# Three moves in the recurrent stage of a two-layer graph kernel

## Chip, cores and metric

One core of a Trainium2 chip runs the whole program. The metric is the device time in microseconds of one execution; the profile shows one such execution, engine by engine. The engines are TensorE (PE in the profile; its weight loads PEld), VectorE (DVE), ScalarE (ACT), GpSimd (POOL) and SyncE (SP), which here only issues DMAs.

## The reference

16 graphs of 1024 nodes, 128 features and a dense 1024 x 1024 adjacency matrix. A layer norm with a ReLU goes ahead of each of two networks, and each result is added to its input. The first network, in which the change lies, is a gated recurrent one of four layers:

```python
for i in range(L):                                   # L = 4
    hw = jnp.einsum('bnc,cd->bnd', h, weight[i])
    m = jnp.einsum('bjn,bjd->bnd', adj, hw)
    h = _gru_cell(m, h, w_ih[i], w_hh[i], b_ih[i], b_hh[i])

# _gru_cell, with gx = m @ w_ih.T + b_ih and gh = h @ w_hh.T + b_hh, each split in three
r = jax.nn.sigmoid(xr + hr)
z = jax.nn.sigmoid(xz + hz)
n = jnp.tanh(xn + r * hn)
return (1.0 - z) * n + z * h
```

The second network has four layers of adjacency times features times weights, a ReLU and a batch norm over all graphs.

## The kernel before

The first network takes about 1170 us of the span, the second the rest. In the first, two streams, `sa` with the even graphs and `sb` with the odd ones, are worked alternately. `half_step(one, two)` (L1035) does two things on TensorE: the gates of stream `two` for its layer (`gate_step(0)` and `gate_step(1)`, a half of 512 nodes each), and then the aggregation over the adjacency matrix of stream `one` (`agg_step(0)` and `agg_step(1)`). `one.i` and `two.i` are the layers at which the streams stand. Both streams need eight half steps for a pair of graphs; seven times a new pair is taken.

The aggregation (L525) multiplies exact adjacency rows with features split in two: a high part, rounded to the matmul's type, and a low part, the remainder. For each block of 128 nodes the two high matmuls come first and the two low ones next, so both parts of a half are wanted at the start. From layer 1 on the features are the state h, which must first be turned by 128 x 128. This is done without TensorE: VectorE turns 32 x 32 blocks (`half_away`, L711, tile `t_h`), SP writes the half to DRAM (`exchange_out`, L591, `cross_h`) and reads it back in four DMAs in the other order of blocks (`exchange_in`, L598, `n_h`), ScalarE makes the high part (`split_back`, L905, `ghw`), VectorE the low part (L906).

In the gates, ScalarE makes r (L984), VectorE two steps of the candidate (L985, L986), ScalarE its tanh (L990) and z (L991), and VectorE three steps of the new h (L995 or L997, L998, L999). z needs the last of the six matmuls of a half. `m` is the aggregation's result, copied by ScalarE (L944).

After its fourth layer a stream takes its next graph (`finish`, L1004). Then the new features `y` and the last state h both go through the same exchange: they are written away at once, and read back in the half step after, `ins` (the new features) at its start, `outs` (the last h, eight DMAs `h<-cross_out`) after the first half of the gates. The last h read back is summed with x under a mask at L732 for the second network's layer norm; the sums, the normed blocks (`y_mid`) and the blocks of the coming graph (`y_in`, `next_blocks`, L818, eight ScalarE instructions from L674) run as work for the gap between the two halves of an aggregation ("gap" in the agenda, `at` and `due`).

The order on TensorE, GpSimd and SP is that of the program text. On ScalarE and VectorE a scheduler puts the instructions in order when the program is built, with durations of its own; `behind(x)` tells it to put what is in its scope behind x, and is an order in the queue, not a wait. `split_back` puts the high part behind the z of the first half, and nothing puts it ahead of or behind the z of the second.

GpSimd rounds adjacency rows (`row`) and casts them to 16 bits (L609, `half`); SP turns these by DMA transposes (L610, `adjT<-half`), and two `half` buffers make the next cast wait for a transpose.

Of the kernel before, what the change touches and what calls it, by code (L numbers as in the profile page):

```python
# [8 lines left out]
F32 = mybir.dt.float32  # L9
# [4 lines left out]
AF = mybir.ActivationFunctionType  # L14
ALU = mybir.AluOpType
AX = mybir.AxisListType
P = 128
# [324 lines left out]
def exact_path(  # L342
# [21 lines left out]
    nc = tc.nc  # L364
    B, N, C = x.shape
    L = g_weight.shape[0]
    NB = N // P
    NH = N // HALF
    BH = HALF // P
# [164 lines left out]
    with ExitStack() as st:  # L534
# [137 lines left out]
        def norm_blocks(xt, y, nt, ks):  # L672
            for k in ks:
                nc.scalar.activation(  # L674
                    y[:, k * P : (k + 1) * P], xt[:, k, :], AF.Relu, bias=nt[3][:, k, :], scale=nt[2][:, k, :]
                )
# [84 lines left out]
        def behind(*inss):  # L761

            es = ExitStack()
            for ins in () if written[0] else inss:
                es.enter_context(tc.issue_after(ins.ins))
            return es

        class Stream:
# [46 lines left out]
            def next_factors(self):  # L815
                norm_factors(self.next_norm)

            def next_blocks(self):  # L818
                self.next_y = work.tile([P, N], F32, tag=f"y{self.tag}", name=f"y_in{self.b + 2}", bufs=1)
                norm_blocks(self.next_x, self.next_y, self.next_norm, range(NB))  # L820

            def plan(self, n, tail=None):

                if tail:
                    b, xt, hT, parts = tail
                    end = {}

                    def sums():
                        end["norm"] = tail_sums(b, xt, hT, parts)

                    def blocks():
                        end["y"] = y_mid(b)
                        norm_blocks(xt, end["y"], end["norm"], range(NB))

                    at(n + 2, "gap", sums)
                    at(n + 3, "mid", lambda: store_xmid(b, xt))
                    at(n + 3, "gap", lambda: norm_factors(end["norm"]))
                    at(n + 4, "gap", blocks)
                    at(n + 5, "mid", lambda: store_ymid(b, end["y"]))
                if self.b + 2 < B:  # L840
                    at(n + 5, "mid", self.next_load)
                    at(n + 5, "gap", self.next_sums)
                    at(n + 6, "gap", self.next_factors)
                    at(n + 7, "gap", self.next_blocks)

            def fetch(self):
# [105 lines left out]
                hin = self.hT[:, :HALF]  # L952
                nc.tensor.matmul(self.opened[2], w_hhT[:, 0, 2 * C : 3 * C], hin, start=True, stop=True)

            def gate_step(self, hf, between=None, after=()):
                i, nm = self.i, f"{self.b}_{self.i}_{hf}"
                if hf == 0 and not self.opened:
                    self.new = work.tile([P, N], F32, tag="h", name=f"h{nm}", bufs=7)
                cols = slice(hf * HALF, (hf + 1) * HALF)
                hin, m = self.hT[:, cols], self.m[hf]  # L960
                across = self.across and i == 0
                if across:
                    hin = by_nodes(hin)
                pr, pz, phn, pxn = self.opened or (
                    tmp(f"{t}{nm}") if written[0] and hf and t == "g_r" else acc(t, f"{t}{nm}")
                    for t in ("g_r", "g_z", "g_hn", "g_xn")
                )

                def part(po, wT, g, rhs, start, stop):
                    if rhs is hin and across:  # L970
                        po = four_ways(po)
                    nc.tensor.matmul(po, wT[:, i, g * C : (g + 1) * C], rhs, start=start, stop=stop)  # L972

                part(pr, w_hhT, 0, hin, True, False)
                part(pr, w_mT, 0, m, False, True)
                if not self.opened:
                    part(phn, w_hhT, 2, hin, True, True)
                part(pxn, w_mT, 2, m, True, True)
                part(pz, w_hhT, 1, hin, True, False)
                part(pz, w_mT, 1, m, False, True)  # L980
                self.opened = None
                r = work.tile([P, HALF], F32, tag="r", name=f"r{nm}")
                z = work.tile([P, HALF], F32, tag="z", name=f"z{nm}")
                self.first_act = nc.scalar.activation(r, pr, AF.Sigmoid, bias=brz[:, 3 * i : 3 * i + 1])  # L984
                nc.vector.scalar_tensor_tensor(r, phn, b_hn(i), r, ALU.add, ALU.mult)  # L985
                self.mid_dve = nc.vector.tensor_add(r, pxn, r)  # L986
                if between:
                    between()
                with behind(*after[:1]):
                    nc.scalar.activation(r, r, AF.Tanh, bias=b_in(i))  # L990
                self.last_act = nc.scalar.activation(z, pz, AF.Sigmoid, bias=brz[:, 3 * i + 1 : 3 * i + 2])  # L991
                ho = self.new[:, cols]
                with behind(*after[1:]):
                    if across:
                        nc.vector.tensor_sub(four_ways(ho), hin, four_ways(r))  # L995
                    else:
                        nc.vector.tensor_sub(ho, hin, r)  # L997
                nc.vector.tensor_mul(ho, ho, z)  # L998
                self.last_dve = nc.vector.tensor_add(ho, ho, r)  # L999
                if hf == NH - 1:  # L1000
                    self.hT = self.new
                    self.i += 1

            def finish(self):  # L1004

                if self.i < L:
                    return
                args = self.b, self.xt, self.hT
                self.b, self.i = self.b + 2, 0
                if self.b >= B:  # L1010
                    self.rest = last_tail(*args)
                    return
                ins = self.take()
                h_in = self.hT
                outs = blocks_out(args[-1], f"out{args[0]}")
                parts = [args[-1][:, hf * HALF : (hf + 1) * HALF] for hf in range(NH)]

                def arrive(ds, ts):
                    for d, t in zip(ds, ts):
                        exchange_in(d, t)  # L1020

                at(clock[0] + 1, "ins", lambda: arrive(ins, [h_in[:, :HALF], h_in[:, HALF:]]))
                at(clock[0] + 1, "outs", lambda: arrive(outs, parts))
                self.plan(clock[0], (*args, parts))

        clock = [3]

        def at(n, place, go):
            agenda.setdefault((n, place), []).append(go)

        def due(place):
            for go in agenda.pop((clock[0], place), ()):
                go()

        def half_step(one, two, gated=None, halfway=None):  # L1035

            feed.next_step()
            one.split = []
            if one.i == 0:
                two.fetch()  # L1040
            due("ins")
            if one is sb and one.i == 0 or written[0] and one is sa:
                feed.jobs = transposes([(s.b, s.rows) for s in (sa, sb)])
            if one.i > 0:
                one.split_step()
                two.fetch()
                feed.some(2)
            two.gate_step(0)
            two.half_away(0)
            two.first_four()  # L1050
            if feed.full or (clock[0], "mid") in agenda:

                pace = small.tile([P, 1], F32, tag="pace", name=f"pace{clock[0]}")
                nc.gpsimd.tensor_copy(pace, two.new[:, :1])
                feed.store()
                due("mid")
            due("outs")
            one.split_back(0, two.last_act, two.mid_dve)
            one.split_back(1, two.last_act, two.mid_dve)
            if one.i > 0:  # L1060
                feed.some(1)
            two.gate_step(1, None, one.split)
            two.half_away(1)
            with behind(two.first_act):
                due("late")
            if one.i == 0:
                feed.some(1)
            two.last_four()
            if gated:
                gated()  # L1070
            if one.i == 0:
                with behind(two.last_m):
                    one.split_step()
            one.agg_step(0)
            if halfway:
                halfway()
            with behind(two.last_act, two.last_dve, *one.split):
                due("gap")
            feed.some(NB if written[0] and one is sa else 1)
            one.agg_step(1)  # L1080
            two.finish()
            clock[0] += 1
# [424 lines left out]
```

## Time and profile before

| | us |
|---|---|
| median of three runs | 1796.18 |
| lowest and highest | 1793.61, 1801.1 |
| profiled execution | 1796.9 |
| its span | 1795.0 |
| idle time of TensorE in the span (1795.0 less 1763.4 busy) | 31.6 |

An undisturbed half step takes 17.57 us on TensorE: 24 records of gate matmuls and 32 of the aggregation. The first row of each answer of a timeline or of waits is left out here; a row has the start, the duration, the queue (an engine, or its sequencer with a q), the line, the operation, output and inputs by name, shape, how many instructions were merged, and in brackets how long the engine stood idle before it and what released it. All times in a timeline are from the span's start. A matmul's drawn end is modelled and runs into the next one, so the distance between starts says more than idle time.

### The profile page before, as it was taken

Reading aid. Unit: us, or ns where it says so; the run is one execution under the profiler, and the core shown is the slowest. Engines: PE = TensorE matmul, PEld = TensorE weight load, DVE = VectorE, ACT = ScalarE, POOL = GpSimd, SP = SyncE. Lnnn points to the kernel's source line nnn. Section 1 sums busy time; section 2 is a strip of 40 time slices with the busy share of each in tenths; the row PEclk is TensorE's granted clock in tenths of the full one; section 3 lists DMA queues with packets and bytes.
Section 4 is the critical chain, followed back from the end, with each engine's and each line's share of the span. In section 5 each row is a group of like instructions: output and inputs, shape, how many; then the busy total and the mean of one; then the engine's idle time right before and its main releaser. Section 6 shows DMA issues by size and latency. Waiting matters only on the chain. (4 is left out here: it accounts for less than half of the span.)

```text
span 1795.0 us, 22286 instructions
## 1 busy us (share of the span) xinstructions
PE 1763.4 (98%) x6742; PEld 1194.0 (67%) x6742; DVE 1258.8 (70%) x2308; ACT 1107.2 (62%) x1717; POOL 389.4 (22%) x417
## 2 busy tenths in 40 slices
PE   9999999999999999999999999999999999999997
PEld 6555565556565556556556555677778888888886
DVE  7567867867776776777786776676666666666665
ACT  5346456556556555755655655477777767768765
POOL 4213322332332331422342333110100000000011
PEclk9999999999999999999999999999999999999999
DMA  7448676776676766766767667778866566767667
GB/s 253 112 125 268 171 223 237 200 207 225 205 211 211 236 191 193 263 197 168 263 185 209 241 194 209 268 277 299 284 223 244 209 244 215 246 223 240 241 220 263
DMA packets 363968, 399.11 MB, mean 222 GB/s; under 512 B 159820, under 2 KB 240496, under 8 KB 363840
## 3 DMA queue, kind: packets, MB, share of 16 engines
q1 hardware_dynamic: 343088, 322.54, 57.1%
q0 software_dynamic: 20224, 74.80, 11.5%
q8 instruction: 55, 0.90, 0.2%
q14 instruction: 73, 0.60, 0.1%
q10 hardware_dynamic: 528, 0.26, 0.0%
HBM read 266.95 MB, written 96.99 MB: 203 GB/s over the span
## 5 line engine op out<-in xcount | busy, mean ns | idle before, releaser
L525 PE MATMUL pm<-row,ghw 128*128 128x512 f32 x2048 | 505.6, 403 | 11.8 <-ACT ghw L905 11.1
L525 PEld LDWEIGHTS pm<-row,ghw 128*128 128x128 f32 x2048 | 384.3, 189 | 124.5 <-issue 26.5
L525 PE MATMUL pc_m<-wide,chw 128*128 128x512 f32 x1024 | 246.1, 396 | 0.0
L609 POOL CAST half<-row 128x1024 bf16<-128x1024 f32 x128 | 148.8, 1171 | 327.2 <-DMA adjT<-half 312.5
L525 PEld LDWEIGHTS pc_m<-wide,chw 128*128 128x128 f32 x1024 | 190.5, 188 | 42.3 <-issue 4.3
L991 ACT ACTIVATE z<-g_z,brz 128x512 f32<-128x512 f32 x128 | 87.5, 684 | 171.3 <-PE g_z L972 171.2
L525 PE MATMUL pc_g_r<-wide,chw 128*128 128x512 f32 x464 | 187.0, 403 | 0.3 <-ACT chw L502 0.3
L578 POOL CAST row<-stage 128x1024 fp32r<-128x1024 f32 x112 | 131.5, 1181 | 243.6 <-DMA stage<-in_adj_dram 221.1
L525 PE MATMUL pc_g_z<-wide,chw 128*128 128x512 f32 x464 | 181.0, 390 | 0.0
L985 DVE SCALAR_TENSOR_TENSOR r<-g_hn,vecs,r 128x512 f32<-128x512 f32 x128 | 95.0, 742 | 118.3 <-ACT r L984 76.6
L1237 DVE CAST wide<-block 128x1024 fp32r<-128x1024 bf16 x160 | 109.8, 692 | 73.2 <-PE pc_m L525 46.2
L1237 DVE CAST wide<-packed 128x1024 fp32r<-128x1024 bf16 x160 | 110.2, 691 | 72.1 <-PE pc_g_z L525 53.9
L944 ACT COPY m<-pm 128x512 f32<-128x512 f32 x128 | 68.5, 586 | 147.9 <-PE pm L525 147.9
L990 ACT ACTIVATE r<-r,vecs 128x512 f32<-128x512 f32 x128 | 91.8, 717 | 104.0 <-DVE r L986 104.0
L997 DVE TENSOR_TENSOR h<-h,r 128x512 f32<-128x512 f32 x96 | 81.8, 852 | 101.6 <-ACT r L990 101.6
L1235 ACT CAST wide<-packed 128x1024 fp32r<-128x1024 bf16 x96 | 100.6, 1048 | 59.1 <-PE pc_m L525 28.3
L972 PE MATMUL g_r<-m,w_mT 128*128 128x512 f32 x256 | 131.5, 595 | 2.8 <-ACT m L944 2.3
L1235 ACT CAST wide<-block 128x1024 fp32r<-128x1024 bf16 x96 | 100.6, 1049 | 52.3 <-PE pc_g_z L525 27.7
L972 PE MATMUL g_xn<-m,w_mT 128*128 128x512 f32 x256 | 130.7, 592 | 0.0
L972 PE MATMUL g_z<-m,w_mT 128*128 128x512 f32 x256 | 130.7, 592 | 0.0
L998 DVE TENSOR_TENSOR h<-h,z 128x512 f32<-128x512 f32 x128 | 118.7, 931 | 4.8 <-ACT z L991 1.9
L1285 DVE BATCH_NORM_STATS2 stats<-feat 128x6 f32<-128x512 f32 x128 | 84.1, 686 | 47.0 <-ACT feat L1284 45.9
(187 smaller groups left out, 2804.3 us busy)
## 6 DMA issues: line engine op xcount, KB each, us to landing
block<-adjT_d SPq DMA_DIRECT2D x256, 256.0 KB, 4.7
packed<-adjT_d SPq DMA_DIRECT2D x256, 256.0 KB, 5.5
stage<-in_adj_dram SPq DMA_DIRECT2D x120, 512.0 KB, 4.8
adjT_d<-adjT POOLq DMA_DIRECT2D x16, 2048.0 KB, 8.3
cross_h<-t_h SPq DMA_DIRECT2D x90, 256.0 KB, 3.2
n_h<-cross_h SPq DMA_DIRECT2D x360, 64.0 KB, 2.0
xmid_d<-x POOLq DMA_DIRECT2D x16, 512.0 KB, 5.4
y<-ymid_d POOLq DMA_DIRECT2D x16, 512.0 KB, 5.9
```

What stands on the lines that cost most here:

```text
L525: nc.tensor.matmul(pm[hf], hw[s][:, j * P : (j + 1) * P], rows[j][:, hf * HALF : (hf + 1) * HALF], start=(j == 0 and s == 0), stop=(j == N ...
L578: nc.gpsimd.tensor_copy(t, stage[j % 4])
L609: nc.gpsimd.tensor_copy(t, row.bitcast(F32))
L972: nc.tensor.matmul(po, wT[:, i, g * C : (g + 1) * C], rhs, start=start, stop=stop)
L985: nc.vector.scalar_tensor_tensor(r, phn, b_hn(i), r, ALU.add, ALU.mult)
L990: nc.scalar.activation(r, r, AF.Tanh, bias=b_in(i))
L991: self.last_act = nc.scalar.activation(z, pz, AF.Sigmoid, bias=brz[:, 3 * i + 1 : 3 * i + 2])
L997: nc.vector.tensor_sub(ho, hin, r)
L998: nc.vector.tensor_mul(ho, ho, z)
L1235: nc.scalar.copy(r, t)
L1237: nc.vector.tensor_copy(r, t)
L1285: nc.vector.bn_stats(stats[:, b * NH + hf, :], dst)
```

## The change

Three moves; no arithmetic is added or taken away.

1. The eight reads of the last h of `sb` (`outs`) move by one half step: they are issued not after the first half of `sa`'s exchange of layer 1 has been written away, but in the half step after, behind the reads of `sa`'s turned h (`n_h`). For `sa` they stay where they were.
2. In the half step where `one` is `sa` with i = 1, the z of the second half of `sb`'s gates is put behind the high part of the first half.
3. For `sb`, four of the eight blocks of the coming `y_in` are put on ScalarE behind the r of the first half of `sa`'s gates, ahead of its z, and four stay in the gap of that half step.

```diff
+            def open_y(self):
+                self.next_y = work.tile([P, N], F32, tag=f"y{self.tag}", name=f"y_in{self.b + 2}", bufs=1)
+                if self is sb:
+                    norm_blocks(self.next_x, self.next_y, self.next_norm, range(BH))
+
             def next_blocks(self):
-                self.next_y = work.tile([P, N], F32, tag=f"y{self.tag}", name=f"y_in{self.b + 2}", bufs=1)
-                norm_blocks(self.next_x, self.next_y, self.next_norm, range(NB))
+                norm_blocks(self.next_x, self.next_y, self.next_norm, range(0 if self is sa else BH, NB))
...
+                    at(n + 7, "early", self.open_y)
                     at(n + 7, "gap", self.next_blocks)
...
-            def gate_step(self, hf, between=None, after=()):
+            def gate_step(self, hf, between=None, after=(), ahead=()):
...
-                self.last_act = nc.scalar.activation(z, pz, AF.Sigmoid, bias=brz[:, 3 * i + 1 : 3 * i + 2])
+                with behind(*ahead):
+                    self.last_act = nc.scalar.activation(z, pz, AF.Sigmoid, bias=brz[:, 3 * i + 1 : 3 * i + 2])
...
-                at(clock[0] + 1, "outs", lambda: arrive(outs, parts))
+                n, place = (1, "outs") if self is sa else (2, "outs behind")
+                at(clock[0] + n, place, lambda: arrive(outs, parts))
...
             if one.i > 0:
                 one.split_step()
+                due("outs behind")
                 two.fetch()
                 feed.some(2)
             two.gate_step(0)
+            with behind(two.first_act):
+                due("early")
             two.half_away(0)
...
             one.split_back(0, two.last_act, two.mid_dve)
+            ahead = one.split[:1] if one is sa and one.i == 1 else ()
             one.split_back(1, two.last_act, two.mid_dve)
...
-            two.gate_step(1, None, one.split)
+            two.gate_step(1, None, one.split, ahead)
```

In the built programs TensorE's and GpSimd's queues are the same before and after. On SP only the eight reads stand elsewhere. On ScalarE and VectorE the scheduler also puts some instructions in another place around these, in the half steps of layers 1 and 2.

## The prediction

> **What bounds the kernel now.** I read the page's table of engines first.
>
> ```profile
> PE 1763.4 (98%) x6742; PEld 1194.0 (67%) x6742; DVE 1258.8 (70%) x2308; ACT 1107.2 (62%) x1717; POOL 389.4 (22%) x417
> ```
>
> TensorE is busy for 98% of the span. None of its instructions is touched, so only its waits can shrink or grow. The second view is TensorE's waits (who is waited for, microseconds in total, times, longest).
>
> ```profile
> PE pm L525 <- ACT ghw L905: 11.1, 7, 2.8
> ...
> PE g_r L972 <- ACT m L944: 2.3, 3, 1.0
> ```
>
> Seven waits of an aggregation for a high part: one for each taking of a new pair of batches, always where `sa` has i = 1. I call that place stage A, and the next half step, where `sb` has i = 1 and `sa` gates, stage B. Third, the timelines of stage A of the third pair, for SP, VectorE, ScalarE and TensorE (start, us, queue, instruction, idle before and its releaser).
>
> ```profile
> 479.92 3.73 SPq L598 DMA_DIRECT2D h<-cross_out  x8
> 483.74 0.38 SPq L591 DMA_DIRECT2D cross_h<-t_h  x1
> 484.25 2.63 SPq L610 DMA_TRANSPOSE adjT<-half  x2
> 486.93 4.07 SPq L598 DMA_DIRECT2D n_h<-cross_h  x8
> ```
>
> ```profile
> 487.35 1.41 DVE L998 TENSOR_TENSOR h<-h,z 128x512 f32<-128x512 f32 x1
> ...
> 490.73 0.70 DVE L711 STREAM_TRANSPOSE t_h<-h 128x512 f32<-128x512 f32 x1
> 491.62 0.69 DVE L906 TENSOR_TENSOR ghw<-n_h,ghw 128x512 fp32r<-128x512 f32 x1 [0.20 <-ACT ghw L905]
> ```
>
> ```profile
> 490.39 0.69 ACT L991 ACTIVATE z<-g_z,brz 128x512 f32<-128x512 f32 x1 [2.75 <-PE g_z L972]
> 490.98 0.61 ACT L905 CAST ghw<-n_h 128x512 fp32r<-128x512 f32 x1
> ```
>
> ```profile
> 489.33 1.02 PE L972 MATMUL g_z<-m,w_mT 128*128 128x512 f32 x2
> 491.64 7.83 PE L525 MATMUL pm<-row,ghw 128*128 128x512 f32 x32 [1.28 <-ACT ghw L905]
> ```
>
> ScalarE stands 2.75 us before z, which cannot start before the gates' last matmul; the high part is queued behind z, and the aggregation behind the high part. Stage B, 17 us later, has the other order and no wait (ScalarE, then TensorE):
>
> ```profile
> 506.29 0.60 ACT L905 CAST ghw<-n_h 128x512 fp32r<-128x512 f32 x1
> 506.80 0.68 ACT L984 ACTIVATE r<-g_r,brz 128x512 f32<-128x512 f32 x1
> 507.38 0.61 ACT L905 CAST ghw<-n_h 128x512 fp32r<-128x512 f32 x1
> 509.81 0.69 ACT L991 ACTIVATE z<-g_z,brz 128x512 f32<-128x512 f32 x1 [1.82 <-PE g_z L972]
> ```
>
> ```profile
> 508.75 1.02 PE L972 MATMUL g_z<-m,w_mT 128*128 128x512 f32 x2
> 509.20 2.16 PE L525 MATMUL pm<-row,ghw 128*128 128x512 f32 x7
> ```
>
> From the last g_z row to the first pm row it is 0.45 us in B and 2.31 in A: A loses 1.86, more than the 1.28 marked, since the g_z end is drawn long. Taken so from TensorE's timeline, whole stages A lose 3.78, 2.48, 1.84, 1.84, 1.83, 1.85 and 3.37: 17.0 us. The first is 1.86, 0.33 of wait for the low part, and 1.6 because the granted clock fell to 0.70 from 206 to 210 us; it did so in one of seven.
>
> **Stage A, the eight reads moved on SP.** `h<-cross_out` (8 issues, 3.73 us) goes from ahead of the second `cross_h` write to behind the eight `n_h` reads. That write then waits only for its t_h, which ends at 480.05 (the two transposes take 1.29 from 478.76). SP: write 480.1, the two DMA transposes 480.5 to 483.1, `n_h` from 483.2 instead of 486.93. Its first four issues end about 485.2 and land a median 2.0 later: 487.3. The moved reads take 487.3 to 491.0, so the next DMA transposes leave at 491.1 as now, and nothing later on SP is pushed. The reads land by 493; their reader, the masked sum at L732, runs on VectorE at 499.03. Cover is 6 us, so this costs 0; without it VectorE would stand, not TensorE.
>
> **Stage A, the high part ahead of z.** ScalarE ends r at 487.65, makes the high part until 488.3, then z at 490.39 as before. TensorE wants it at 489.33 + 0.45 = 489.78: met with 1.5 us to spare. But two matmuls later it wants the low part, and VectorE's order here is not changed: behind the transpose at 490.73 its turn would come about 491.42, were the data there. That would leave the whole wait in place. It shortens by what leaves VectorE's chain: L998 takes 1.41 beside GpSimd's cast at 487.10, against a median of 0.692, and L999, at 489.35, takes 0.85 beside the cast at 488.55, against 0.691. GpSimd's queue keeps its order, but these casts wait for the DMA transposes, which go 3.7 us earlier, so they come at 483.4 and 484.9, beside L985 and L986. Those read PSUM and never stretch (longest of 128: 751 and 693 ns). So the low part ends at 492.11 - 0.72 - 0.17 = 491.22. Now it ends 0.67 behind the first pm matmul without a second wait, so 0.67 is free: 491.22 - 489.78 - 0.67 = 0.77 lost. Six stages at 0.77 and the last, whose VectorE chain is 1.4 later (transpose at 1064.94 against 1063.35 for the pm start), at 2.1: 6.7 us. Bounds: 0, if the low part is never late, and 7 x 1.86 = 13.0, if the stretch stays. I take 6.7, as the cast's move follows from SP's rows. Gain 17.0 - 6.7 = 10.3, bounds 4.0 and 17.0.
>
> **Stage B, what the reordering does besides.** ScalarE's and VectorE's order is the scheduler's. In the built program of the changed kernel, ScalarE's queue in B is r, z, tanh, r, z, high, high, tanh, in all seven pairs; the profile's order is r, z, tanh, high, r, high, z, tanh. So B gets A's old order: the second z cannot start before 509.81 (g_z), the high part then runs 510.40 to 511.0 and TensorE starts at 511.05 instead of 509.20: 1.85 us, as in the four plain stages A. VectorE's low part is behind its transpose, which ends about 510.4, so it follows the high part at once as in A and adds nothing. Behind the waiting z on ScalarE are the second high part and tanh (to 512.3), eight y_mid blocks (3.2 us), a table load (1.28) and the square root (0.30): they end about 517.1, and the m copy they precede is due at 516.84 + 1.85 = 518.7, so nothing further is late. 7 x 1.85 = 13.0. Bounds: 0, were the queue's order not to bind, and 7 x 3.37 = 23.6, the longest A. I take 13.0: the z row waits for PE in every stage.
>
> **Clock.** One of seven such waits lost 1.6 to the clock; seven new ones of the same length: +1.6, bounds 0 and 7 x 1.6 = 11.2. The Trainium skill, "TensorE: Matmul & The Clock Gate", section "Why this matters for your kernels", lets a matmul stream keep its clock through gaps up to about 3 us, so by it this term is 0 and the sum 1.6 lower; the fall at 206 us after a 1.28 us wait disagrees.
>
> **Half of y_in.** Where `sa` gates layer 3, the ScalarE timeline of the sixth pair has
>
> ```profile
> 871.33 3.18 ACT L674 ACTIVATE y_in<-x,ms_in,rs_in 128x128 f32<-128x128 f32 x8
> 874.42 1.03 ACT L944 COPY m<-pm 128x512 f32<-128x512 f32 x2
> ```
>
> and TensorE's second g_r waits for m. In the seven half steps after such blocks the gates take longer than the usual 9.44 by 0.23, 0.83, 0.39, 0.39, 0.62, 1.42 and 1.43; 0.33 of the 0.83 is a wait for z. Four blocks less are 4 x 0.39 = 1.6 us, more than any of these: gain 5.0, bounds 0 and 5.3. The four moved blocks (1.6 us) stand between r and z, where ScalarE stands 2.31 us for g_z ahead of the z at 860.82: covered, at 0; without the cover they would hold up z and behind it VectorE, which TensorE does not wait for there.
>
> **Sum.** 1796.9 (span 1795.0 and 1.9 around it) - 10.3 - 5.0 + 13.0 + 1.6 = 1796.2. That run is 0.7 above the median of 1796.18, so I forecast 1795.5: the wait moves from the first stream to the second, and the rest nearly cancels. A measurement of this kernel tells about 0.5% (9 us) from no change.
>
> **Rivals.** *No new wait:* B runs on as now, and the text does what it says. Its reads are ready at 506.29, well ahead of z; against it is the built order. 1795.5 - 13.0 - 1.6 = 1780.9. *VectorE still holds A:* the casts stretch other SBUF operations and the low part comes as late as now; for it L998 and L995 stretch to 1.5 wherever a cast falls. 1795.5 + 13.0 - 6.7 = 1801.8, slower; it decides once the low part ends behind 491.3. *The clock falls after each wait in B:* place 511 to 515, 1.6 each; slower from the second fall on, with seven 1795.5 + 9.6 = 1805.1. Against it: six of seven stages A had a clock of 1.00.
>
> **How the numbers follow.** Forecast 0.72, no new wait 0.10, VectorE 0.12, clock 0.06. Below 1787 lies the first rival and a tail of the forecast: 0.14; above 1805 half the clock's case and the tails: 0.10; between 0.76. The range must hold the forecast's bounds and VectorE's case and leaves most of the first and last outside: 1786 to 1803.
>
> **What would show it.** In the changed profile, TensorE's waits should show pm <- ACT ghw about 1.28 seven times, now with `sa`'s gates ahead, pm <- DVE ghw small in stage A, and g_r <- ACT m only once (0.3). SP's `n_h` should start 3.7 us earlier and L998 in A last 0.69. No wait in B, or A's wait undiminished, makes me wrong.

## The result and the profile after

| | before | after |
|---|---|---|
| median of seven runs, us | 1797.25 | 1807.48 |
| lowest and highest | 1793.61, 1801.1 | 1801.44, 1809.62 |
| profiled execution | 1796.9 | 1806.62 |
| its span | 1795.0 | 1804.8 |

The changed kernel takes 1.0054 of the time before (95% interval 1.0042 to 1.0066): some 10 us longer, where 0.7 us less had been forecast, and above the range of 1786 to 1803.

The first view of the changed kernel is its page's table of engines (busy us, share, instructions).

```profile
PE 1768.9 (98%) x6742; PEld 1195.6 (66%) x6742; DVE 1256.4 (70%) x2308; ACT 1107.7 (61%) x1717; POOL 379.9 (21%) x417
```

The second is TensorE's waits, after (total us, times, longest).

```profile
PE pm L525 <- ACT ghw L910: 9.0, 7, 1.3
PE pm L525 <- DVE ghw L911: 7.9, 11, 1.9
...
PE g_z L977 <- ACT z L997: 1.6, 6, 0.6
PE g_hn L977 <- DVE r L990: 1.2, 3, 0.5
...
PE g_r L977 <- ACT m L949: 0.3, 1, 0.3
```

The instructions are the same in number, but TensorE's busy time grew by 5.5 us, which with equal work means a lower clock somewhere. There are still seven waits for the high part, now all in stage B, 1.28 each. The wait for the low part (L911) was 0.3 in all before and is 7.9 now, and its longest, 1.9, exceeds any of the waits for the high part. The wait of the gates for `m` fell from 2.3 to 0.3, but two others, for z and for VectorE's r, stand in its place.

Waits alone leave out the drawn ends and the clock. So I took each stage's loss from the distance between starts in TensorE's timeline, less that of an undisturbed half step (9.44 for its gates, 8.13 for its aggregation). For the seven pairs of batches, in us:

| | stage A | stage B | gates behind `y_in` |
|---|---|---|---|
| before | 17.0 | 0 | 5.3 |
| after, by pair | .65 .61 .70 .61 .61 .61 1.98 | 1.84 2.37 1.85 5.24 4.11 4.41 1.85 | .01 1.56 1.49 .63 1.44 .59 .37 |
| after, sum | 5.8 | 21.7 | 6.1 |

A gives 11.2, B takes 21.7, the gates behind `y_in` take 0.8 more: +11.3. The span grew by 9.8, so 1.5 was won outside these stages (0.6 of it in the prelude, 0.8 from the last gates of the first network on). No edit lies there, and the eleven profiles of this document differ by as much in these two stretches (84.8 to 85.6 us and 630.5 to 632.2 us).

Stage A of the third pair, after, as timelines of SP, ScalarE, VectorE and TensorE:

```profile
483.69 3.86 SPq L598 DMA_DIRECT2D n_h<-cross_h  x8
487.95 3.67 SPq L598 DMA_DIRECT2D h<-cross_out  x8
```

```profile
487.71 0.61 ACT L910 CAST ghw<-n_h 128x512 fp32r<-128x512 f32 x1
490.55 0.69 ACT L997 ACTIVATE z<-g_z,brz 128x512 f32<-128x512 f32 x1 [2.24 <-PE g_z L977]
```

```profile
487.60 0.69 DVE L1004 TENSOR_TENSOR h<-h,z 128x512 f32<-128x512 f32 x1
...
490.06 0.70 DVE L711 STREAM_TRANSPOSE t_h<-h 128x512 f32<-128x512 f32 x1
490.69 0.65 DVE L911 TENSOR_TENSOR ghw<-n_h,ghw 128x512 fp32r<-128x512 f32 x1
```

```profile
489.50 1.02 PE L977 MATMUL g_z<-m,w_mT 128*128 128x512 f32 x2
489.95 1.03 PE L525 MATMUL pm<-row,ghw 128*128 128x512 f32 x2
```

The first two pm matmuls start 0.45 behind the last g_z row, as if nothing were wanted. The high part was made 2.8 us before z. What is left of A is the low part, which ends at 491.34, behind VectorE's transpose.

Stage B of the fifth pair, after (ScalarE, VectorE, GpSimd, TensorE):

```profile
800.39 0.69 ACT L997 ACTIVATE z<-g_z,brz 128x512 f32<-128x512 f32 x1 [2.69 <-PE g_z L977]
800.97 1.13 ACT L910 CAST ghw<-n_h 128x512 fp32r<-128x512 f32 x2
```

```profile
801.61 1.42 DVE L911 TENSOR_TENSOR ghw<-n_h,ghw 128x512 fp32r<-128x512 f32 x1 [1.08 <-ACT ghw L910]
```

```profile
801.83 0.89 POOL L743 DMA_DIRECT2D xmid_d<-x  x1
802.71 2.66 POOL L609 CAST half<-row 128x1024 bf16<-128x1024 f32 x2
```

```profile
801.63 0.72 PE L525 MATMUL pm<-row,ghw 128*128 128x512 f32 x2 [1.28 <-ACT ghw L910]
803.08 6.14 PE L525 MATMUL pm<-row,ghw 128*128 128x512 f32 x19 [0.72 <-DVE ghw L911]
```

This is the whole of the loss in one place. ScalarE stands for z with the high part behind it (the forecast). VectorE does start the low part at once, but it takes 1.42 instead of the 0.65 of stage A, beside GpSimd's write of x and its cast (the DMA issue and the casts in GpSimd's rows). So TensorE stops a second time, for 0.72. Then its clock falls: 19 matmuls take 6.14, where an undisturbed 32 take 7.83, and so a window over 6 us reads (window, length, busy time and instructions of PE, PEld, DVE, ACT, POOL, then clock, DMA share, GB/s):

```profile
801.00:807.00 6.00, 4.64 (x13) 3.41 (x14) 5.32 (x5) 5.98 (x13) 4.36 (x4) 0.72 0.89 350
```

Over the seven pairs, B's 21.7 divides into 13.0 for z and the high part, 4.1 for the second wait (0.52, 1.92, 0.72 and 0.94 in pairs 2, 4, 5 and 6) and 4.6 for a lower clock in pairs 4, 5 and 6 (1.47, 1.54 and 1.62).

### The profile page after: what moved, and what is told of

Its sections match the earlier page's. It is cut to its first block, busy times and chain, and to the rows that moved or that the text cites. A ratio compares the mean times of both kernels' runs of the same rounds, so it can differ in the third digit from the quotient of the medians.

```text
span 1804.8 us, 22321 instructions
## 1 busy us (share of the span) xinstructions
PE 1768.9 (98%) x6742; PEld 1195.6 (66%) x6742; DVE 1256.4 (70%) x2308; ACT 1107.7 (61%) x1717; POOL 379.9 (21%) x417
## 3 DMA queue, kind: packets, MB, share of 16 engines
q0 software_dynamic: 20224, 74.80, 11.4%
## 5 line engine op out<-in xcount | busy, mean ns | idle before, releaser
L609 POOL CAST half<-row 128x1024 bf16<-128x1024 f32 x128 | 143.5, 1129 | 324.4 <-DMA adjT<-half 309.7
L990 DVE SCALAR_TENSOR_TENSOR r<-g_hn,vecs,r 128x512 f32<-128x512 f32 x128 | 95.1, 743 | 136.8 <-ACT r L989 86.6
L1003 DVE TENSOR_TENSOR h<-h,r 128x512 f32<-128x512 f32 x96 | 77.9, 811 | 97.8 <-ACT r L995 97.8
L989 ACT ACTIVATE r<-g_r,brz 128x512 f32<-128x512 f32 x128 | 88.0, 688 | 38.8 <-PE g_r L977 38.4
```

Of the source, the lines that this page charges most:

```text
L609: nc.gpsimd.tensor_copy(t, row.bitcast(F32))
```

## The experiments

The theory after the result: move 1 makes the scheduler turn ScalarE's order in B; the turned order costs 13.0 by itself; GpSimd's work beside the low part makes the second wait, and the second wait the fall of the clock. In the gates behind `y_in`, VectorE's reductions were the next to be late. Rivals were that B's order comes from move 2 or 3, that the low part is late for its own order alone, and that in those gates z is held up by the moved blocks. All ratios are to the kernel before; a line number without a name is that of the changed kernel.

**The high part ahead of z in both streams.** All three moves, with

```diff
-            ahead = one.split[:1] if one is sa and one.i == 1 else ()
+            ahead = one.split[:1] if one.i == 1 else ()
```

> The changed kernel, with z put behind the high part in both streams' layer-1 half steps. Theory (z ahead of the high part in stage B costs 1.28 marked and 1.85 real each, and the rest of B's 21.6 us follows from it): TensorE's wait pm <- ACT ghw disappears (0 of 7, from 9.0 us); what stays in B is the low part behind VectorE's transpose, 0.8 to 1.6 a pair, 6 to 11 us in all; about 1794 us (1790 to 1798). Rival (the low part alone sets stage B, the high part's place does not matter): pm <- DVE ghw takes over, B keeps 1.85 or more a pair, 1803 us or above.

Measured: 1791.43, ratio 0.9964 (0.9951 to 0.9978). Stage B loses 5.4 instead of 21.7; A loses 7.9, with a fall of the clock in the last pair. In TensorE's waits the high part is gone, and the low part is the first row:

```profile
PE pm L525 <- DVE ghw L911: 7.2, 14, 2.0
```

The one line of order in B is worth 16 us of the median. Of B's 21.7, 16.3 is the queue order on ScalarE and what follows from it; 5.4 stays with the low part.

**One move at a time.** Each is the kernel before with one move. Move 1 alone (the reads on SP):

> Only the eight reads of the second stream's last h moved on SP; no z put behind a high part, no half of y_in moved. Theory (the move on SP is what makes the scheduler turn z and the high part round, in both stages): stages A near 0.6 to 0.8 each, stages B 1.85 and more each, as in the changed kernel; 1807 us (1803 to 1810). Rival (the other two moves bring the loss): stage B as in the kernel before, 1786 to 1792 us.

Move 2 alone (`ahead` in stage A):

> Only z behind the high part for the first stream; reads and y_in as before. Theory (in stage A the data come too late for the order to matter: n_h issued at 486.93, landed about 491): stages A keep 1.8 to 2.5 each, stages B lose nothing; 1797 us (1794 to 1800). Rival (the order alone removes stage A's wait): 1786 us.

Move 3 alone (half of `y_in`):

> Only half of y_in between r and z. Theory (the m wait goes and VectorE's reductions ahead of r take its place at once): g_r <- ACT m only once, gates behind y_in still 4 to 6 us over their usual time in all, 1796.5 us (1795 to 1798). Rival (the prediction's term): 5.0 us less, 1792 us.

| | median, us | ratio, 95% | A | B | behind `y_in` |
|---|---|---|---|---|---|
| move 1 | 1810.17 | 1.0071 (1.0057 to 1.0085) | 5.8 | 20.8 | 6.5 |
| move 2 | 1796.83 | 0.9995 (0.9986 to 1.0004) | 18.2 | 0 | 6.7 |
| move 3 | 1797.18 | 0.9997 (0.9988 to 1.0007) | 16.2 | 0 | 6.4 |

Of move 1 alone, TensorE's waits:

```profile
PE pm L525 <- ACT ghw L910: 9.0, 7, 1.3
PE pm L525 <- DVE ghw L911: 8.8, 13, 1.9
```

They are close to those of the changed kernel. Move 1 brings both A's gain and B's loss, with no instruction about z in its text: in the built program the scheduler now puts the high part ahead of z in A and behind z in B. Presumably it counts on the turned h at another time; its own times are not on record. Move 2 asks for an order in A that move 1 already brings. Alone, it leaves the median as it was: the reads still stand ahead of `n_h` on SP, and the high part, now ahead of z, waits 3.28 for the data (TensorE's waits, and ScalarE in stage A of the third pair):

```profile
PE pm L525 <- ACT ghw L910: 8.5, 6, 2.8
```

```profile
491.01 0.62 ACT L910 CAST ghw<-n_h 128x512 fp32r<-128x512 f32 x1 [3.28 <-DMA n_h<-cross_h]
```

Its waits for the two parts are 10.1 together, against 11.4 before; the 18.2 of A is larger than 17.0 because the clock fell in two of its stages, against one before.

Move 3 alone moves no sum; it swaps one wait for others, as below.

**The low part ahead of the candidate too.** All three moves, `ahead` in both streams, and on VectorE the low part ahead of the second half's first step:

```diff
-                nc.vector.scalar_tensor_tensor(r, phn, b_hn(i), r, ALU.add, ALU.mult)
+                with behind(*ahead[1:]):
+                    nc.vector.scalar_tensor_tensor(r, phn, b_hn(i), r, ALU.add, ALU.mult)
...
-                with behind(*ahead):
+                with behind(*ahead[:1]):
...
-            ahead = one.split[:1] if one is sa and one.i == 1 else ()
+            ahead = one.split if one.i == 1 else ()
```

> As e1_both_ahead, and the second half's first VectorE step (L990, adding the bias to g_hn) put behind the low part of the first half in both streams, which brings the low part two VectorE instructions (1.35 us) forward. Theory (what is left in stages A and B, 0.6 to 0.7 each, is the low part's place in VectorE's queue): both stages near 0 but for the last pair, pm <- DVE ghw from 7.2 us to below 2, about 1783 us (1780 to 1786). Rival (it only delays the second half's h, and a wait of the same size opens behind it): 1790 us or above.

Measured: 1781.63, ratio 0.9914 (0.9898 to 0.9929); A 1.5, B 0.2. The profiled execution, 1786.06, is the slowest of the four: it loses 4.6 outside both stages, in one half step of the last pair, by a single wait of 1.56 for a high part and a fall of the clock behind it. Stage B of the third pair (ScalarE, VectorE, TensorE by start):

```profile
500.21 0.61 ACT L910 CAST ghw<-n_h 128x512 fp32r<-128x512 f32 x1
...
503.00 0.69 ACT L998 ACTIVATE z<-g_z,brz 128x512 f32<-128x512 f32 x1 [2.18 <-PE g_z L977]
```

```profile
502.06 0.65 DVE L911 TENSOR_TENSOR ghw<-n_h,ghw 128x512 fp32r<-128x512 f32 x1
```

```profile
502.40 7.83 PE L525 MATMUL pm<-row,ghw 128*128 128x512 f32 x32
```

All 32 matmuls in one row without a wait. With the reads moved, both stages can be almost free at once. So the data were no longer what was late: the order on two queues was.

**GpSimd's work out of stage B's way.** The changed kernel, but in B the copy that paces GpSimd, with the writes and casts behind it, waits for the second half of h instead of the first:

```diff
-            if feed.full or (clock[0], "mid") in agenda:
-                pace = small.tile([P, 1], F32, tag="pace", name=f"pace{clock[0]}")
-                nc.gpsimd.tensor_copy(pace, two.new[:, :1])
-                feed.store()
-                due("mid")
+            later = one is sb and one.i == 1 and not written[0]
+            def mid(col):
+                if feed.full or (clock[0], "mid") in agenda:
+                    pace = small.tile([P, 1], F32, tag="pace", name=f"pace{clock[0]}")
+                    nc.gpsimd.tensor_copy(pace, two.new[:, col : col + 1])
+                    feed.store()
+                    due("mid")
+            if not later:
+                mid(0)
...
             two.half_away(1)
+            if later:
+                mid(HALF)
```

> The changed kernel, with GpSimd's pace copy and the two stores and casts behind it waiting in stage B for the second half's h instead of the first's; all queues else as in the changed kernel. Theory (the casts and stores fall on VectorE's low part in B, stretch it, and the second wait that makes brings the clock down): pm <- DVE ghw small in stage B, no fall of the clock there, B 7 x 1.85 = 13 instead of 21.7 us, about 1799 us (1797 to 1802). Rival (the low part is long for another reason, and the clock falls from the z wait alone): B 18 us or more, 1805 or above.

Measured: 1799.81, ratio 1.0017 (1.0008 to 1.0026). B loses 12.9, 1.84 or 1.85 in each pair. The fifth pair again (VectorE, GpSimd, TensorE, and the window):

```profile
797.83 1.29 DVE L911 TENSOR_TENSOR ghw<-n_h,ghw 128x512 fp32r<-128x512 f32 x2 [1.08 <-ACT ghw L910]
```

```profile
801.24 0.19 POOL L1066 COPY pace<-h 128x1 f32<-128x1 f32 x1 [9.34 <-DVE h L1005]
```

```profile
797.85 7.83 PE L525 MATMUL pm<-row,ghw 128*128 128x512 f32 x32 [1.28 <-ACT ghw L910]
```

```profile
800.00:806.00 6.00, 6.00 (x28) 4.73 (x26) 2.75 (x5) 4.12 (x10) 3.98 (x5) 1.00 0.52 190
```

With nothing of GpSimd beside them both low parts take 1.29 together, there is one wait and not two, and the clock is 1.00. The 13.0 of the forecast is what remains; the other 8.8 hung on GpSimd's place.

**The reductions behind `y_in`.** In the half steps behind `y_in`, VectorE has four reductions over raw adjacency rows (`look`, L604), which test whether 16 bits hold them exactly. The timeline of VectorE and TensorE of the changed kernel, second pair:

```profile
299.31 2.33 DVE L604 TENSOR_REDUCE low<-stage 128x1 f32<-128x1024 uint16 x2
...
303.89 1.21 DVE L604 TENSOR_REDUCE low<-stage 128x1 f32<-128x1024 uint16 x1
305.02 0.73 DVE L990 SCALAR_TENSOR_TENSOR r<-g_hn,vecs,r 128x512 f32<-128x512 f32 x1
```

```profile
305.81 1.12 PE L977 MATMUL g_hn<-h,w_hhT 128*128 128x512 f32 x2 [0.48 <-DVE r L990]
...
308.33 1.13 PE L977 MATMUL g_z<-h,w_hhT 128*128 128x512 f32 x2 [0.20 <-ACT z L997]
```

VectorE comes to L990 late, the tanh and the z behind it on ScalarE are late with it, and TensorE waits for the room that these would have freed. Two kernels leave `sa`'s reductions out (so a part of the exactness test is missing): the kernel before, and the kernel before with move 3.

```diff
-                    with behind(self.last_dve):
-                        for j in range(4, NB):
-                            look(b, stage[j % 4], j)
+                    return
```

> The kernel before, without the first stream's four reductions (L604) that look at the low bits of adjacency rows 4 to 7 of its coming graph; that part of the exactness flag is left out. Theory (in the half step after y_in TensorE waits for m behind y_in on ScalarE, and VectorE's reductions are the next limit close behind): without them alone m is as late as before, gates there 4 to 6 us long in all, 1796 us (1793 to 1798). Rival (VectorE's reductions are the limit already): 1791 us.

> As e7_no_looks_before, with half of y_in between r and z (move 3 alone). Theory: with the reductions gone the move gets its 5 us: gates after y_in below 1 us long in all, 1791 us (1789 to 1793), 4 to 6 us below e7_no_looks_before. Rival (the reductions are not what took the gain): same as e7_no_looks_before within 1 us.

| | median, us | ratio, 95% | behind `y_in` |
|---|---|---|---|
| before, without the reductions | 1794.13 | 0.9985 (0.9976 to 0.9994) | 6.0 |
| the same with move 3 | 1788.49 | 0.9958 (0.9944 to 0.9971) | 0.0 |

Without the reductions move 3 is worth 5.6 us of the median, and its whole 6.0 in those gates; with them, nothing. Both medians came some 2 us below what was expected: stage A, too, lost less (16.0 and 14.1 against 17.0), which had not been foreseen. In the first of the two the old wait stands alone:

```profile
PE g_r L970 <- ACT m L942: 4.2, 5, 1.0
```

**All of it together.** The version with high and low part ahead in both streams, and of the four reductions two left on VectorE and two done by ScalarE (`glance`) behind the copies of `m`. Its diff to the former of these:

```diff
-                self.outs, self.split = [], []
+                self.outs, self.split, self.pend = [], [], None
...
-                        for j in range(4, NB):
+                        for j in range(4, 6):
                             look(b, stage[j % 4], j)
+                    self.pend = lambda: glance(b, stage, range(6, NB))
...
             one.agg_step(1)
+            if two.pend:
+                with behind(one.last_m):
+                    two.pend()
+                two.pend = None
             two.finish()
```

> As e5_low_ahead, and two of the first stream's four reductions (rows 6 and 7) moved from VectorE to ScalarE, behind the m copies. Theory (VectorE's reductions ahead of r take the gain of the y_in move): the half steps after y_in lose 1 to 2 us in all instead of 6.5; about 1777 us (1774 to 1780). Rival (ScalarE then holds r or tanh up, and the loss stays): 1781 us or above.

Measured: 1776.96, ratio 0.9900 (0.9883 to 0.9918), span 1774.4; A 1.0, B 0.5, behind `y_in` 0.0. All that TensorE's waits still have of these stages:

```profile
PE pm L525 <- DVE ghw L912: 0.7, 1, 0.7
...
PE g_r L978 <- ACT m L950: 0.6, 2, 0.3
```

It is faster than both kernels, and with the whole of the computation.

## Why the prediction was wrong, step by step

The difference of 12.0 between the median and the forecast is +7.1 from stage B with its clock (21.7 against 13.0 and 1.6), +5.8 from `y_in` (a loss of 0.8 against a gain of 5.0) and -0.9 from stage A. The 1.5 won outside the stages is offset by the median itself: the forecast set it 0.7 below the profiled run, and it came 0.9 above (1807.48 against 1806.62).

- **Stage A: right.** 6.7 was forecast, 5.8 measured, the last pair 1.98 for 2.1. `n_h` came 3.2 us earlier (3.7 was forecast), L1004 (L998 before) took 0.69, and the residue is the low part behind the transpose, as worked out. The masked sum that reads the moved data held up nothing.
- **Stage B, z ahead of the high part: right in mechanism and size.** 13.0 forecast; 1.84 to 1.85 in each pair where GpSimd was out of the way.
- **Stage B, "so it follows the high part at once as in A and adds nothing": the step that failed first.** The low part did start at once, but it was priced by the row of A, where GpSimd was idle. In the third pair of the kernel before, B's low parts ran from 507.10 to 508.98, ahead of the pace copy at 509.65; held back behind z they fall into the writes and casts that follow this copy. The forecast had used just this stretch in A, on L998, and did not ask for it in B. 4.1 us.
- **Clock: under-sized, and counted by the wrong thing.** 1.6 was forecast for one fall in seven; there were three, 4.6. I had counted the first waits, all of 1.28; with GpSimd's work out of the way, seven of these alone brought no fall. In the changed kernel the three falls came where a second wait followed, but a second wait neither decides nor is needed. With move 1 alone, 1.28 and 0.94 brought no fall in two pairs, and 1.28 and 0.68 none in another. Single waits brought one after 1.56 and 2.81 (move 2 alone), 1.72 (before, without the reductions) and 1.95 (high part ahead of z in both streams). So three of seven is in part luck; what the falls have in common is in the last section. Of the page of the Trainium skill that the forecast weighed ("TensorE: Matmul & The Clock Gate", section "Why this matters for your kernels"), the wait of 2.80 without a fall in the kernel before agrees with its bound of about 3 us; the falls behind single waits of 1.56 to 2.81 do not.
- **`y_in`: the step "four blocks less are 1.6 us, more than any of these: gain 5.0" failed.** The wait for `m` did go, from 2.3 to 0.3. But behind it VectorE's reductions were nearly as late, and took its place. The row for z that the forecast met there (0.33 of the 0.83) was the sign of it. The moved blocks themselves cost nothing that shows: with the reductions gone, the same blocks in the same place lose 0.0. The loss of 0.8 is itself no more than these gates differ between profiles without move 3 (5.3 before, 6.5 and 6.7 with move 1 or 2 alone).
- **The rivals.** The slower one that named the clock had the right place and direction, but rested on a fall after every first wait. No rival had the second wait.

What is not settled is how much each of GpSimd's operations holds up the low part, and why the scheduler turned the order in B.

## What to carry to other kernels

Where a scheduler orders some queues, read the order of the built program at every place that uses the moved data, not only at the place that was edited: here a move on one DMA queue turned two instructions on another engine, a half step later, and that cost 16 of the 21.7 us lost there. When work is pushed later, look at what the other engines do in the window that it is pushed into, and price it by a row that had the same neighbours. A wait that goes is worth its length less that of the runner-up in the same gap; find the second latest input before booking the gain.

## What the runs showed of the hardware

- What the clock went by in these profiles is TensorE's idle time within fixed intervals of 3.41 us, not the length of one wait. Between the first warm clock and the last matmuls the granted clock is either 1.00 or 0.50, and a fall lasts 3.41 us, or twice that. In the changed kernel the falls start at 656.17, 802.94 and 949.72, in the fifth pair so (window, length, TensorE busy, clock, DMA share, GB/s):

```profile
799.53:802.94 3.41, 1.54 (x4) 1.00 0.44 159
802.94:806.36 3.42, 3.28 (x8) 0.50 1.02 398
```

  These starts lie 146.77 and 146.78 apart, 43 times 3.413 each, so I laid such intervals over all eleven profiles, counted from a fall in each (that at the end, where there is no other). All seven intervals with 1.73 us or more of marked idle time were followed by a fall, three of six with 1.56 to 1.66, and none with less. So a wait of 1.56 that lay in one interval brought a fall (move 2 alone, second pair, below), and one of 2.80 that was cut into 1.25 and 1.55 did not (before, last pair). It is inferred from ten falls; no run tested it by shifting a wait across a boundary.

```profile
346.97 6.24 PE L525 MATMUL pm<-row,ghw 128*128 128x512 f32 x18 [1.56 <-ACT ghw L910]
```

```profile
348.71:352.13 3.42, 3.42 (x9) 0.50 0.59 158
```

- VectorE's sum of two SBUF operands (128x512, f32) can be held up for nearly as long as GpSimd casts beside it. The low part took 0.65 alone and 2.61 in the fourth pair, 1.96 more, beside two casts of 2.02 together:

```profile
653.75 2.61 DVE L911 TENSOR_TENSOR ghw<-n_h,ghw 128x512 fp32r<-128x512 f32 x1 [1.08 <-ACT ghw L910]
```

```profile
653.78 2.02 POOL L609 CAST half<-row 128x1024 bf16<-128x1024 f32 x2
```

  The second low part of the third pair took 3.40 beside an issue (0.89) and two casts. Whether GpSimd's issue of a DMA counts too stays open: in the fifth pair the low part took 1.42 beside one issue (0.89) and the first 0.3 us of a cast, but in the third pair 0.69 beside two issues.
